# Seven smaller blocks in place of one: the A12 B21 product of a two-level Winograd scheme, with its operand sums on GpSimd

## The chip, the cores and the metric

The kernel runs on one core of one Trainium2 chip. The metric is the device time of one execution in microseconds (us). Matrix products run on TensorE (PE; its weight loads are listed as PEld), elementwise work on VectorE (DVE), ScalarE (ACT) and GpSimd (POOL); DMA transfers are issued from the queue of SyncE (SP). All data is fp32. TensorE writes into PSUM; VectorE and ScalarE take results out of it.

## The reference

Eight batches x[b] of 256 tokens by 1024 features go through two chained products and a residual:

```python
y = einsum('bsi,boi->bso', x, weight[adapter_ids])          # one 1024x1024 matrix per batch
base_out = einsum('btd,od->bto', y, base_W) + base_b        # the same matrix for all batches
logits = einsum('btd,nd->btn', y, router_W) + router_b      # 15 routes; softmax, all ranked, the first 8 kept
h = einsum('btd,erd->bter', y, A)                           # 8 experts of rank 16
lora = einsum('bter,eor->bto', h * w[..., None], B) * 2.0   # w: the weights of the kept routes, mapped to experts
out = x + base_out + lora
```

## The kernel before

**Two phases.** The first computes y, batch by batch, and beside it router and low-rank projections (`project`, L135). The second, from 228 us on, computes the product with base_W for all batches at once, with the low-rank term and the residual added. Both use the Winograd form of Strassen's scheme: a product of two 2 x 2 block matrices made with seven block products instead of eight, at the price of sums of blocks.

**The second phase has two levels.** The outer level is seven products, `seven`, numbered n = 0 to 6 here; the call for n = 6 is `last_product`, the others are `product`. Their right operands are quarters of y held in SBUF: `b11`, `b21`, `b12`, `b22`, some changed in place beforehand by the outer sums (`update`, L812; which product issues which sums is in `sums`). Their left operands (blocks of base_W and sums of them) were prepared in DRAM and are loaded a product ahead by `load_left` (L208, L212), which needs free tiles of the pool `wt` (8 buffers).

**The inner level** is again seven block products, of (256 x 256) by (256 x 1024), hence four matmuls of 128x512 each: left blocks `a11`, `a12`, `a22` and sums `s1` to `s4`, which come from DRAM; right blocks `b11` to `b22` of that product and sums `t1` to `t4`, which VectorE makes (`differences`, L232). Products 1, 3, 5 and 6 also add the low-rank term: inside four of their blocks, two more matmuls each (L587). `half` is one bank's part of a block (L578 for its matmuls). The trace lists every fp32 matmul as two records, so a block of four matmuls shows as x8.

**PSUM and the order of the work.** Each product has three pairs of banks: `pa`, `pb`, `pc`. Winograd's running sums stay in the banks: `pa` collects a11 b11, then + s2 t2, then + s3 t3, then + a22 t4; `pc` collects s1 t1, then + s4 b22. After each block the bank is read (`take`, L630 on ACT in product 5, L634 on ACT in product 0, otherwise on DVE at L607 or, with a bias, L636; `join`, L607 on DVE), and the next block that writes the same bank waits for that read. The order on TensorE is the order of the source, since PE, DVE, ACT and SP are scheduled by hand:

```python
block(pa, a11, b11, True)
block(pc, s1, t1, True, *term(1, 1))
block(pa, s2, t2, False)
block(pb, a12, b21, True, *term(0, 0))
block(pa, s3, t3, False)
block(pc, s4, b22, False, *term(0, 1))
block(pa, a22, t4, False, *term(1, 0))
```

**The gaps.** Between the blocks `gap(k)` issues steps from two queues, `soon` and `later`, two or three at a time (`fill`): the differences for the next product, outer sums, steps of the router's softmax, and the residual sums with their stores (L710, L721, L731, L732, L714). Every engine works strictly through its own list, so a step issued in a gap stands ahead of the next read of a bank on DVE. GpSimd has no work after the first 1.4 us.

**Other tiles the change touches.** `q` (pool of 4 tiles) holds results of products 1 and 5 until they are stored. `late` is a large tile that first holds results of phase one (copied out of it by ACT at L312 until 243.9 us), then, from product 3, results (`v`). `spare` of phase one holds prepared left operands until they are stored to DRAM (L348); the pool `q` lies over it. `ys[0]`, `ys[1]` hold y.

Of the kernel before, what the change touches and what calls it, by code (L numbers as in the profile page):

```python
# [10 lines left out]
F32 = mybir.dt.float32  # L11
# [17 lines left out]
def kernel(  # L29
# [16 lines left out]
    nc = tc.nc  # L46
    P = 128
    B = ids.shape[1]
    S = 256
# [20 lines left out]
    NS = 4  # L70
# [134 lines left out]
    def load_left(n):  # L205

        ra = wpool.tile([P, NS, 4 * P], F32, name="wt")
        nc.sync.dma_start(  # L208
            ra.rearrange("p s f -> p (s f)"), left_raw[n].rearrange("p s f -> p (s f)")
        )  # L210
        su = wpool.tile([P, NS, 3 * P], F32, name="wt")
        nc.sync.dma_start(  # L212
            su.rearrange("p s f -> p (s f)"), left_sum[n].rearrange("p s f -> p (s f)")
        )
        return ra, su

    def quarter(right, i, j):

# [22 lines left out]
    left = {}  # L241
# [307 lines left out]
    with ExitStack() as phase:  # L549
# [9 lines left out]
            tc.tile_pool(name="ps_b", bufs=1, space=bass.MemoryType.PSUM)  # L559
        )  # L560
        phase.enter_context(
            tc.manual_schedule(engines={EN.PE, EN.DVE, EN.Activation, EN.SP})
        )
        add, sub = nc.vector.tensor_add, nc.vector.tensor_sub
        W = 2 * S
# [4 lines left out]
        def fill(n):  # L570
            for _ in range(n):
                if soon or later:
                    (soon or later).popleft()()
# [33 lines left out]
                add(dst[:, mi], accs[mi], base[:, mi])  # L607

        def operands(left, right):
            ra, su = left  # L610
            return (
                [ra[:, :, ts(n, P)] for n in range(4)]
                + [su[:, :, ts(n, P)] for n in range(3)]
                + [quarter(right, i, j) for i in range(2) for j in range(2)]
            )

        def product(left, terms, nexts, right, base, bias, into, done, gaps, u=None, hw=None):

            a11, a12, s3, a22, s1, s2, s4, b11, b12, b21, b22 = operands(left, right)
            t1, t2, t3, t4 = terms

            def take(dst, accs, i, j):
                if bias is None and base is not None:
                    join(dst, accs, base(i, j))
                    return
                for mi in range(2):
                    if bias is None:
                        nc.scalar.copy(dst[:, mi], accs[mi])  # L630
                        continue
                    c = bb[:, bias + 2 * i + mi : bias + 2 * i + mi + 1]
                    if base is None:
                        nc.scalar.activation(dst[:, mi], accs[mi], AF.Identity, bias=c)  # L634
                    else:
                        nc.vector.scalar_tensor_tensor(  # L636
                            dst[:, mi], accs[mi], c, base(i, j)[:, mi], ALU.add, ALU.add
                        )

            def term(i, j):  # L640
                if u is None:
                    return ()
                t = hw[:, j].rearrange("p b t -> p (b t)")
                return (upd[:, u, :] if (i, j) == (0, 1) else up[:, u, i, :]), t

            def gap(n, more=0):
                for step in gaps.get(n, ()):
                    step()
                fill(3 if more and u is not None else 2)

            pa, pb, pc = banks(ps_a, "pa"), banks(ps_b, "pb"), banks(ps_b, "pc")
            c = {ij: into(*ij) for ij in ((0, 0), (1, 1), (0, 1), (1, 0))}
            gap(0)
            block(pa, a11, b11, True)
            take(c[0, 0], pa, 0, 0)
            gap(1, 1)
            block(pc, s1, t1, True, *term(1, 1))
            take(c[1, 1], pc, 1, 1)
            gap(2)
            block(pa, s2, t2, False)  # L660
            take(c[0, 1], pa, 0, 1)
            gap(3, 1)
            block(pb, a12, b21, True, *term(0, 0))
            join(c[0, 0], pb, c[0, 0])
            done(0, 0, c[0, 0])
            gap(4)
            block(pa, s3, t3, False)
            join(c[1, 1], pa, c[1, 1])
            done(1, 1, c[1, 1])
            gap(5, 1)  # L670
            block(pc, s4, b22, False, *term(0, 1))
            join(c[0, 1], pc, c[0, 1])
            done(0, 1, c[0, 1])
            gap(6, 1)
            block(pa, a22, t4, False, *term(1, 0))
            take(c[1, 0], pa, 1, 0)

            while len(nexts) < 4:
                fill(1)
            done(1, 0, c[1, 0])  # L680

        def fresh(i, j):
            return qpool.tile([P, 2, W], F32, name="q")
# [5 lines left out]
            pass  # L689

        u = mpool.tile([P, 2, 2, 2, W], F32, name="u")


        results = [(0, 0), (1, 1), (0, 1), (1, 0)]
# [42 lines left out]
        def last_product(left, terms, right, r, res, u, hw):  # L737


            a11, a12, s3, a22, s1, s2, s4, b11, b12, b21, b22 = operands(left, right)  # L740
            t1, t2, t3, t4 = terms
            pa, pb, pc, pd = (
                banks(p, x) for p, x in ((ps_a, "pa"), (ps_b, "pb"), (ps_b, "pc"), (ps_a, "pa"))
            )
            xl = []

            def ask_all():

                for i in range(2):
                    t = wpool.tile([P, 2, 2 * W], F32, name="wt")  # L750
                    n = number(*r, i, 0)
                    nc.sync.dma_start(t, xr[n : n + 2].rearrange("n p f -> p n f"))
                    xl.append(t)

            def multiply(accs, left, right, first, ij=None):
                t = ()
                if ij is not None:
                    t = (
                        upd[:, u, :] if ij == (0, 1) else up[:, u, ij[0], :],
                        hw[:, ij[1]].rearrange("p b t -> p (b t)"),  # L760
                    )
# [13 lines left out]
            ask_all()  # L775
            multiply(pa, a11, b11, True)
            fill(2)
            take(pa, 0, 0)
            multiply(pc, s1, t1, True, (1, 1))
            fill(3)  # L780
            take(pc, 1, 1)
            multiply(pa, s2, t2, False)
            fill(2)
            take(pa, 0, 1)
            multiply(pc, s4, b22, False, (0, 1))
            fill(3)
# [12 lines left out]
            for acc, mi, at in (  # L799
                (pb[0], 0, ds(0, W)),  # L800
                (pb[1], 1, ds(0, 2 * q)),
                (pd[0], 1, ds(2 * q, q)),
                (pd[1], 1, ds(3 * q, q)),
            ):
                dst = res[:, 0, 0, mi, at]
                half(acc[:, at], mi, a12, b21, True, up[:, u, 0, :], t, at)
                add(dst, acc[:, at], dst)
                nc.sync.dma_start(to[:, mi, at], dst)

        def update(dst, op, x, z, halves=(0, 1)):  # L810
# [12 lines left out]
            (b12, at(u), None, at(u), nothing),  # L823
            (b22, at(u), None, at(v), nothing, 2, hw2),
            (b11, at(u), KH, at(u), nothing),
            (b12, None, None, fresh, joint, 1, hw2),
            (b21, at(u), None, at(u), None, 1, hw1),
        ]

        sums = {  # L830
            0: update(b12, sub, b22, b12, [0]) + update(b12, add, b12, b11, [0]),
            2: update(b11, sub, b12, b11),
            3: update(b21, sub, b21, b12) + update(b12, sub, b22, b12),
        }

        def project_last():
# [9 lines left out]
        for n, (right, base, bias, into, done, *up_hw) in enumerate(seven):  # L846
# [3 lines left out]
            if not last:  # L850
                gaps[0].append(lambda m=n + 1: left.update({m: load_left(lefts[m])}))
                steps = [
                    (lambda s=s: nexts.append(s())) for s in differences(seven[n + 1][0])
                ]
                gaps[0].append(lambda o=steps + sums.get(n, []): soon.extend(o))
            if n == 0:
                for k, count in ((1, 6), (2, 5), (3, 11)):
                    gaps[k].append(lambda count=count: run(behind, count))
# [17 lines left out]
            product(  # L876
                left.pop(n), terms, nexts, right, base, bias, into, done, gaps,
                *(up_hw or (None, None))
            )
            terms = nexts  # L880
# [65 lines left out]
```

## Time and profile before

| | us |
|---|---|
| median of 3 runs (lowest, highest) | 432.93 (432.42, 433.91) |
| the profiled execution | 432.58 |
| its span | 430.8 |
| PE, PEld busy | 425.6, 209.0 |
| DVE, ACT, POOL busy | 327.0, 163.5, 0.7 |
| first matmul of product 0; last matmul's start | 227.96; 427.42 |

Products 0 to 6 start on TensorE at 227.96, 255.92, 286.82, 310.85, 341.75, 365.78 and 396.68 us. The times of a timeline are counted from the start of the span; the profiled execution's own time is 1.8 us more than its span. A group's mean is the duration of one record; matmuls overlap their neighbours, so the time that one takes on the path is read from the distance between starts. The granted TensorE clock is full in all 40 slices.

### The profile page before, as it was taken

How to read it: one execution, taken by the hardware profiler on the slowest of the kernel's cores; microseconds unless marked ns; L12 is line 12 of the kernel's file. 1: busy time of each engine (PE TensorE's matmuls, PEld its weight loads, DVE VectorE, ACT ScalarE, POOL GpSimd, SP SyncE). 2: the span in 40 equal slices, each digit the busy share in tenths (PEclk: the TensorE clock that was granted, in tenths of full speed). 3: DMA queues.
4: the chain of work that ended last, by engine and by line, in shares of the span. 5: the costliest groups of instructions: out<-in, count | busy, mean ns of one | idle time of the engine just before them, and what ended most of it. 6: DMA issues, size and time to landing. Idle time of an engine off the chain costs nothing.

```text
span 430.8 us, 3839 instructions
## 1 busy us (share of the span) xinstructions
PE 425.6 (99%) x1198; PEld 209.0 (49%) x1198; DVE 327.0 (76%) x490; ACT 163.5 (38%) x442; POOL 0.7 (0%) x6
## 2 busy tenths in 40 slices
PE   8999999999999999999999999999999999999997
PEld 6344464644646446455455554444444444444444
DVE  0699999986888898998996477879598495446773
ACT  1019377965758657666826632300000000201000
POOL 0000000000000000000000000000000000000000
PEclk9999999999999999999999999999999999999999
DMA  7997987959788589792694241092702227018525
GB/s 253 417 360 269 345 331 294 315 209 309 233 300 285 213 304 347 241 319 104 224 397 160 97 162 58 2 361 102 267 1 99 73 86 277 2 50 278 202 104 196
DMA packets 26406, 93.13 MB, mean 216 GB/s; under 512 B 2322, under 2 KB 6290, under 8 KB 24082
## 3 DMA queue, kind: packets, MB, share of 16 engines
q1 hardware_dynamic: 26242, 92.36, 59.1%
q10 hardware_dynamic: 144, 0.52, 0.4%
q8 instruction: 9, 0.15, 0.1%
q14 instruction: 11, 0.09, 0.1%
HBM read 71.65 MB, written 21.23 MB: 216 GB/s over the span
## 4 chain that ended last, share of the span: by engine, by line
PE 96%; DMA 2%; SPq 1%; issue 0%; DVE 0%
PE pa L294 24%; PE pa L578 23%; PE pc L294 13%; PE pc L578 11%; PE pb L294 7%; PE ph L135 6%; PE pb L578 5%; PE pc L587 3%; DMA wt<-in_wq_dram 2%; PE pa L587 2%; PE pb L587 1%; PE pa L135 1%; SPq L363 0%; DMA ids_sb<-in_ids_dram 0%; SPq L376 0%
## 5 line engine op out<-in xcount | busy, mean ns | idle before, releaser
L312 ACT COPY y<-late 32x256 f32<-32x256 f32 x256 | 103.0, 402 | 41.9 <-DVE late L247 38.9
L578 PE MATMUL pa<-wt 128*128 128x512 f32 x168 | 76.0, 592 | 0.0
L294 PE MATMUL pa<-wt,x 128*128 128x512 f32 x128 | 57.5, 593 | 0.1
L294 PE MATMUL pa<-wt,tt 128*128 128x512 f32 x120 | 54.0, 593 | 0.0
L578 PEld LDWEIGHTS pa<-wt 128*128 128x128 f32 x168 | 31.9, 190 | 40.2 <-issue 38.5
L630 ACT COPY q<-pa 128x512 f32<-128x512 f32 x6 | 3.5, 586 | 114.4 <-PE pa L578 96.7
L294 PEld LDWEIGHTS pa<-wt,x 128*128 128x128 f32 x128 | 24.2, 190 | 30.4 <-issue 29.9
L258 ACT COPY hwT<-late 32x64 f32<-32x64 f32 x128 | 31.1, 243 | 11.2 <-DVE late L247 9.6
L294 PEld LDWEIGHTS pa<-wt,tt 128*128 128x128 f32 x120 | 22.3, 190 | 26.2 <-issue 25.9
L135 PEld LDWEIGHTS ph<-late,y 128*128 128x128 f32 x224 | 28.4, 189 | 3.3 <-issue 3.3
L294 PE MATMUL pb<-wt,x 128*128 128x512 f32 x64 | 29.1, 595 | 0.8 <-DMA wt<-in_wq_dram 0.8
L294 PE MATMUL pc<-wt,x 128*128 128x512 f32 x64 | 28.9, 594 | 0.0
L294 PE MATMUL pc<-wt,tt 128*128 128x512 f32 x64 | 28.8, 592 | 0.0
L135 PE MATMUL ph<-late,y 128*128 128x143 f32 x224 | 28.6, 284 | 0.0
L578 PE MATMUL pa<-y,wt 128*128 128x512 f32 (+1 forms) x64 | 26.4, 552 | 0.0
L578 PE MATMUL pc<-y,wt 128*128 128x512 f32 x56 | 25.8, 592 | 0.0
L578 PE MATMUL pc<-wt 128*128 128x512 f32 x56 | 25.8, 592 | 0.0
L578 PE MATMUL pb<-y,wt 128*128 128x512 f32 (+1 forms) x56 | 25.0, 577 | 0.0
L409 DVE TENSOR_TENSOR wt<-wt 128x2048 f32<-128x2048 f32 (+1 forms) x9 | 18.4, 2047 | 7.9 <-PE pa L294 5.5
L247 DVE STREAM_TRANSPOSE late<-late 128x512 f32<-128x512 f32 (+1 forms) x33 | 21.4, 647 | 1.1
L294 PEld LDWEIGHTS pb<-wt,x 128*128 128x128 f32 x64 | 12.0, 190 | 16.8 <-issue 14.3
L607 DVE TENSOR_TENSOR u<-pa,u 128x512 f32<-128x512 f32 x20 | 13.4, 686 | 8.3 <-PE pa L578 6.8
(101 smaller groups left out, 453.6 us busy)
## 6 DMA issues: line engine op xcount, KB each, us to landing
wt<-in_wq_dram SPq DMA_DIRECT2D x28, 1024.0 KB, 5.8
x<-in_xq_dram SPq DMA_DIRECT2D x7, 1024.0 KB, 7.3
wt<-left_raw SPq DMA_DIRECT2D x7, 1024.0 KB, 6.7
xt<-in_xr_dram SPq DMA_DIRECT2D x12, 512.0 KB, 4.5
wt<-left_sum SPq DMA_DIRECT2D x7, 768.0 KB, 7.2
wt<-in_wq_dram SPq DMA_DIRECT2D x8, 512.0 KB, 7.8
spare<-in_bq_dram SPq DMA_DIRECT2D x4, 1024.0 KB, 5.1
left_raw<-spare SPq DMA_DIRECT2D x4, 1024.0 KB, 7.3
```

The source lines that it names most:

```text
L135: nc.tensor.matmul(ph[:, j, : ER + N], lhsT=y[:, k // KH, k % KH // 2, th, k % 2, bi, ts(j, P)], rhs=ar_sb[:, k, :], start=(j == order[0] ...
L247: nc.vector.transpose(half, of)
L258: lambda a=a, r=r: nc.scalar.copy(to[32 * r : 32 * r + 32, :, a, :], hw[32 * a : 32 * a + 32, :, ts(r, 32)],)
L294: nc.tensor.matmul(acc, lhsT=right[:, k, :], rhs=left[:, k, :], start=(first and k == 0), stop=(k == KH - 1), skip_group_check=True,)
L312: lambda a=a, r=r: nc.scalar.copy(y[32 * r : 32 * r + 32, :, :, a, :], m[32 * a : 32 * a + 32, :, :, r, :])
L409: nc.vector.tensor_add(q["s1"][:, h], q["a21"][:, h], q["a22"][:, h])
L578: nc.tensor.matmul(acc, lhsT=left[:, 2 * k + mi, :], rhs=right[:, k, at], start=(first and k == 0), stop=(up is None and k == 1), skip_gro ...
L587: nc.tensor.matmul(acc, lhsT=up[:, ts(mi, P)], rhs=hw[:, at], start=False, stop=True, skip_group_check=True,)
L607: add(dst[:, mi], accs[mi], base[:, mi])
L630: nc.scalar.copy(dst[:, mi], accs[mi])
```

## The change

In products 0 to 5 the block A12 B21 is made by Winograd's scheme once more. Its quarters are 128x128 (`d11` to `d22`, of `a12`) and 128x256 (`e11` to `e22`, of `b21`); seven products d e of one 128x256 matmul each take the place of four matmuls of 128x512, with the low-rank term joined to three of them (`ups`, three 128x256 matmuls in place of two of 128x512). The running sum `sx` lives in bank `pb[0]`, the other products one after the other in `pb[1]` (`sy`). Each of the seven results is added by DVE to the quarter of c[0, 0] it belongs to as soon as it is there (`small`), where before two sums of 128x512 joined the whole block.

The sums of the small blocks, four of 128x128 and four of 128x256 in each product and one more 128x128 in products with a low-rank term, are made by GpSimd, which joins the engines scheduled by hand. Those of the left side lie in unused columns of the loaded `su` tile, those of the right side in a place that `room` names: a `q` tile in products 0, 3 and 4, part of `late` in 1 and 2, part of `ys[0]` in 5.

The seven small products stand between the large blocks: two behind a11 b11, two behind s1 t1, two behind s2 t2, one ahead of a22 t4. The block s4 b22 is split into its two halves, one ahead of s3 t3 and one behind it. The number of steps per gap becomes `FILLS`. Product 5 now has its right operand in `b22`, and the two outer sums that were issued in product 3 are issued in products 4 and 5, ahead of the differences.

```diff
-        su = wpool.tile([P, NS, 3 * P], F32, name="wt")
+        su = wpool.tile([P, 4 * NS * P], F32, name="wt")
...
-            tc.manual_schedule(engines={EN.PE, EN.DVE, EN.Activation, EN.SP})
+            tc.manual_schedule(engines={EN.PE, EN.DVE, EN.Activation, EN.SP, EN.Pool})
...
-            def gap(n, more=0):
+            def gap(n):
                 for step in gaps.get(n, ()):
                     step()
-                fill(3 if more and u is not None else 2)
+                fill(FILLS[n] + (u is not None))
...
             gap(0)
+            d11, d21, d12, d22 = (a12[:, n] for n in range(4))
+            e11, e12, e21, e22 = (b21[:, k, ts(h, S)] for k in range(2) for h in range(2))
+            ds1, ds2, ds3, ds4 = (left[2][:, n] for n in range(4))
+            et1, et2, et3, et4 = (home[0][:, ts(n, S)] for n in range(4))
+            plus, minus = nc.gpsimd.tensor_add, nc.gpsimd.tensor_sub
+            plus(ds1, d21, d22)
+            minus(et1, e12, e11)
+            minus(ds2, ds1, d11)
+            minus(et2, e22, et1)
+            minus(ds4, d12, ds2)
+            minus(ds3, d11, d21)
+            minus(et3, e22, e12)
+            minus(et4, e21, et2)
+            if u is not None:
+                ups = [up[:, u, 0, ts(mi, P)] for mi in range(2)]
+                ups.append(home[1])
+                minus(ups[2], ups[0], ups[1])
+            sx, sy = (b[:, :S] for b in pb)
+            def small(acc, d, e, first, mi, h, n=None):
+                joins = u is not None and n is not None
+                nc.tensor.matmul(
+                    acc, lhsT=d, rhs=e, start=first, stop=not joins, skip_group_check=True
+                )
+                if joins:
+                    nc.tensor.matmul(
+                        acc, lhsT=ups[n], rhs=hw[:, 0, h], start=False, stop=True,
+                        skip_group_check=True,
+                    )
+                dst = c[0, 0][:, mi, ts(h, S)]
+                add(dst, acc, dst)
             block(pa, a11, b11, True)
             take(c[0, 0], pa, 0, 0)
-            gap(1, 1)
+            small(sx, d11, e11, True, 0, 0)
+            small(sy, d12, e21, True, 0, 0, 0)
+            gap(1)
             block(pc, s1, t1, True, *term(1, 1))
             take(c[1, 1], pc, 1, 1)
+            small(sy, ds1, et1, True, 1, 1, 1)
+            small(sx, ds2, et2, False, 0, 1)
             gap(2)
             block(pa, s2, t2, False)
             take(c[0, 1], pa, 0, 1)
-            gap(3, 1)
-            block(pb, a12, b21, True, *term(0, 0))
-            join(c[0, 0], pb, c[0, 0])
-            done(0, 0, c[0, 0])
+            small(sy, ds4, e22, False, 0, 1, 2)
+            small(sx, ds3, et3, False, 1, 1)
+            gap(3)
+            half(pc[0], 0, s4, b22, False, *term(0, 1))
+            block(pa, s3, t3, False)
             gap(4)
-            block(pa, s3, t3, False)
+            half(pc[1], 1, s4, b22, False, *term(0, 1))
             join(c[1, 1], pa, c[1, 1])
             done(1, 1, c[1, 1])
-            gap(5, 1)
-            block(pc, s4, b22, False, *term(0, 1))
             join(c[0, 1], pc, c[0, 1])
             done(0, 1, c[0, 1])
-            gap(6, 1)
+            gap(5)
+            small(sx, d22, et4, False, 1, 0, 1)
+            done(0, 0, c[0, 0])
             block(pa, a22, t4, False, *term(1, 0))
+            gap(6)
             take(c[1, 0], pa, 1, 0)
...
+        FILLS = (2, 2, 1, 2, 1, 1, 2)
...
+        def room(n):
+            if n in (1, 2):
+                return late[:, : 4 * S], late[:, 4 * S : 4 * S + P]
+            if n == 5:
+                t = ys[0][:, 0].rearrange("p i j k b t -> p (i j k b t)")
+                return t[:, : 4 * S], t[:, 4 * S : 4 * S + P]
+            q = qpool.tile([P, 2, W], F32, name="q")
+            return q.rearrange("p m t -> p (m t)"), late[:, 16 * S : 16 * S + P]
...
-            (b12, None, None, fresh, joint, 1, hw2),
+            (b22, None, None, fresh, joint, 1, hw2),
...
-            3: update(b21, sub, b21, b12) + update(b12, sub, b22, b12),
+            4: update(b22, sub, b22, b12),
+            5: update(b21, sub, b21, b12),
...
-                gaps[0].append(lambda o=steps + sums.get(n, []): soon.extend(o))
+                ahead = sums.get(n, [])
+                gaps[0].append(
+                    lambda o=ahead + steps if n > 3 else steps + ahead: soon.extend(o)
+                )
```

In `last_product` two counts of steps change: all that is left in `soon` behind the first block, and one step instead of three behind s4 b22.

More of the change, by code (lines that the diff above doesn't have):

```diff
@@ L210, in load_left @@
         )
-        su = wpool.tile([P, NS, 3 * P], F32, name="wt")
-        nc.sync.dma_start(
-            su.rearrange("p s f -> p (s f)"), left_sum[n].rearrange("p s f -> p (s f)")
+        su = wpool.tile([P, 4 * NS * P], F32, name="wt")
+        nc.sync.dma_start(su[:, : 3 * NS * P], left_sum[n].rearrange("p s f -> p (s f)"))
+        return (
+            ra,
+            su[:, : 3 * NS * P].rearrange("p (s f) -> p s f", s=NS),
+            su[:, 3 * NS * P :].rearrange("p (n o) -> p n o", n=4),
         )
-        return ra, su
     def quarter(right, i, j):
@@ L609, in operands @@
         def operands(left, right):
-            ra, su = left
+            ra, su, _ = left
             return (
@@ L615, in operands, with product @@
             )
-        def product(left, terms, nexts, right, base, bias, into, done, gaps, u=None, hw=None):
+        def product(
+            left, terms, nexts, right, base, bias, into, done, gaps, home, u=None, hw=None
+        ):
             a11, a12, s3, a22, s1, s2, s4, b11, b12, b21, b22 = operands(left, right)
@@ L776, in last_product @@
             multiply(pa, a11, b11, True)
-            fill(2)
+            fill(max(2, len(soon)))
             take(pa, 0, 0)
@@ L785, in last_product @@
             multiply(pc, s4, b22, False, (0, 1))
-            fill(3)
+            fill(1)
             take(pc, 0, 1)
@@ L876 @@
             product(
-                left.pop(n), terms, nexts, right, base, bias, into, done, gaps,
+                left.pop(n), terms, nexts, right, base, bias, into, done, gaps, room(n),
                 *(up_hw or (None, None))
```

## The prediction

> **What bounds the kernel now.** I read the page first: the busy times and the chain that ended last.
>
> ```profile
> PE 425.6 (99%) x1198; PEld 209.0 (49%) x1198; DVE 327.0 (76%) x490; ACT 163.5 (38%) x442; POOL 0.7 (0%) x6
> PE 96%; DMA 2%; SPq 1%; issue 0%; DVE 0%
> ```
>
> TensorE is the chain: after a first transfer nothing but matmuls, and no other engine has a share behind it. So what is taken from TensorE is won in full, if no new wait opens; what is added elsewhere costs nothing as long as it comes before the block that needs it. Then I read the busy time of each engine in windows, one per product; products 0, 2 and 4 are the short ones.
>
> ```profile
> core 0: us, PE busy (x) PEld busy (x) DVE busy (x) ACT busy (x) POOL busy (x), PEclk, DMA share, GB/s
> 227.96:255.92 27.96, 27.96 (x91) 14.57 (x90) 17.68 (x37) 14.28 (x33) 0.00 (x0) 1.00 0.30 102
> 286.82:310.85 24.03, 24.03 (x58) 10.64 (x56) 19.14 (x23) 0.00 (x0) 0.00 (x0) 1.00 0.58 221
> 341.75:365.78 24.03, 24.03 (x57) 10.64 (x56) 18.52 (x22) 0.00 (x0) 0.00 (x0) 1.00 0.46 158
> ```
>
> TensorE has no idle time in any of them, at full clock; DVE has 5 to 10 us free in each. Next the timeline of TensorE: the block that goes, in product 2 and with its low-rank term in product 1, and, at the very end, the only matmuls of 256 columns.
>
> ```profile
> 267.93 1.88 PE L578 MATMUL pb<-y,wt 128*128 128x512 f32 x4
> 269.65 1.02 PE L587 MATMUL pb<-hwT,up 128*128 128x512 f32 x2
> ...
> 297.12 3.60 PE L578 MATMUL pb<-y,wt 128*128 128x512 f32 x8
> 300.55 3.60 PE L578 MATMUL pa<-wt 128*128 128x512 f32 x8
> ...
> 425.01 1.03 PE L578 MATMUL pb<-y,wt 128*128 128x256 f32 x4
> 425.87 0.59 PE L587 MATMUL pb<-hwT,up 128*128 128x256 f32 x2
> 426.30 0.61 PE L578 MATMUL pa<-y,wt 128*128 128x128 f32 x4
> ```
>
> From start to start, eight records of 512 columns take 300.55 - 297.12 = 3.43 us, 0.429 each; six of 256 take 426.30 - 425.01 = 1.29, 0.215 each. Half the columns cost half the time: the weight load of each (0.190 by the groups' mean) still hides under 0.215. A matmul is two records: 0.858 and 0.429 us. Last, the groups of DVE at the end of the run and GpSimd's own rows.
>
> ```profile
> L732 DVE TENSOR_TENSOR q<-u,q 128x1024 f32<-128x1024 f32 x4 | 4.9, 1222 | 0.1
> L607 DVE TENSOR_TENSOR u<-pb,u 128x512 f32<-128x512 f32 x2 | 1.4, 686 | 0.4 <-PE pb L578 0.4
> L807 DVE TENSOR_TENSOR u<-pa,u 128x128 f32<-128x128 f32 x2 | 0.6, 292 | 0.6 <-PE pa L587 0.6
> L807 DVE TENSOR_TENSOR u<-pb,u 128x256 f32<-128x256 f32 x1 | 0.4, 425 | 0.6 <-PE pb L587 0.6
> ...
> masks.py:199 POOL TENSOR_SCALAR_AFFINE_SELECT ident<-ident 128x128 f32<-128x128 f32 x1 | 0.3, 294 | 0.1
> ```
>
> **TensorE, what goes and comes.** Four matmuls of 512 (3.43 us) go, seven of 256 (7 x 0.429 = 3.00) come: 0.43 less, six times, 2.57. In products 1, 3 and 5 two more of 512 go (1.72) and three of 256 come (1.29): 0.43 less, three times, 1.29. Together 3.86 us. Splitting s4 b22 moves its halves and adds nothing. More matmuls now begin behind a wait; in the trace the first weight load of a block already waits for a release from DVE or ACT, and TensorE's idle time in the second phase is 0.0 on every line, so a wait that is fulfilled in time costs nothing.
>
> **GpSimd's sums.** No row shows them. From below: DVE's row of the same shapes, 0.43 (128x256) and 0.29 us (128x128). From above: GpSimd's own row of 128x128, 0.294 with one input, doubled for a second input and again for 256 columns: 1.18 and 0.59. I take the upper end, since it is from the engine itself. A product's eight sums are then 4 x 1.18 + 4 x 0.59 = 7.1 us, against 23.6 or more per product. [...]
>
> What matters is when they can start. In product 0 et1 goes into a `q` tile over `spare`, so it waits for the last store from there: issued at 225.52, landed 5.8 us later (the median of that issue alone), 231.3. With 1.18 and 0.59, et1 is there at 232.6, ds2 at 233.2, et2 at 234.4. TensorE wants ds1 and et1 behind a11 b11, two small products and s1 t1: 227.96 + 3.43 + 0.86 + 3.43 = 235.7, and ds2, et2 at 236.1. 1.7 us to spare; the later sums are wanted from 240 on. In product 1 they start when ACT has emptied that part of `late` (243.9 before, some 2 us later now, since s2 t2 ends later), 10 us ahead of their product. In products 2 to 5 they wait for the left tile (loads take about 7 us from the end of product n - 2) and for the places to be free, both in the course of product n - 1: a whole product ahead. Only et4 of product 2 waits for the last small product of product 1, and has 20 us after that. So nothing.
>
> **DVE's reads.** Per product two sums of 512 columns (2 x 0.69) go and seven of 256 (7 x 0.43) come: 1.6 us more on an engine with 5 to 10 free. Each stands right behind its matmul. The second result in `sy` is written a whole s1 t1 after the first is read; the same for the others.
>
> **The large banks.** Less stands between the blocks on `pa` now. s3 t3 follows s2 t2 after two small products and half a block, 0.86 + 1.72 = 2.57 us, where 3.43 stood; `take` of c[0, 1] needs 0.65 behind the end of s2 t2: 1.9 to spare. a22 t4 follows s3 t3 after half a block and one small product, 2.15 us; join needs 0.65: 1.5 to spare. DVE must only not be behind. Put in order for product 2 from the end of a11 b11 (take 1.3 with a lag of 0.7, small sums 0.35 each, two differences 1.14 each, take, small sums, one outer sum), DVE is free at 8.6 us, s2 t2 ends at 8.58. Then two small sums and three outer sums fill the time to 13.4, when half of s3 t3 can be joined since 12.9; s3 t3 ends at 14.6. In product 4 the same places come out within 0.2 us. In products 1, 3 and 5 the blocks are 0.86 to 1.72 us longer and the margins wider. Product 0 takes on ACT: s2 t2 ends at 239.98, and take is done 0.7 later, s3 t3 starts at 242.6. So nothing.
>
> **Queues and what moves.** ACT's copies out of `late` end about 1.7 us later (245.6); the projection that reads them starts behind s4 b22, at 247.7 instead of 245.1. The outer sums moved from product 3 to 4 and 5 are the same eight instructions; in product 4 the first two stand in front of take, where DVE was idle 1.9 us at a time at the end of product 3. On SP the loads of left operands for product 3 stand behind two stores instead of three, those of y's residual in the old order but for one request that goes behind the loads for product 6; the last residual tile comes 4.5 us after about 400, read at 404.6, and the bank that hangs on DVE there (c[0, 1] of product 6) is wanted at 410: the read is done at 408.2. The tail behind product 6's a22 t4 is unchanged.
>
> **The sum.** Profiled 432.58 (span 430.8 and 1.78 around it) less 3.86 is 428.7; the median of three was 0.35 above it, 432.93, hence 429.1.
>
> **Rivals.** [...] Nothing in the trace tells whether GpSimd and DVE disturb each other, as GpSimd never ran beside it. As a mechanism here: each step of DVE with both inputs in SBUF (the 1.22 us rows) and each sum of GpSimd hold each other up for their whole length. In products 2 and 4 two or three sums fall on such steps between s1 t1 and s2 t2, 1.2 to 3.5 us later on DVE against 1.9 to spare: 0 to 1.6 lost in each, 429.1 to 432.3, the middle 430.7. [...]
>
> (2) The other side: GpSimd is far slower than its own row says. In product 0, 231.4 and 2.5 times the duration of a 128x256 sum must not pass 236.1. At 1.9 us TensorE begins to wait, at 3.4 the whole gain is gone, at 4 it waits 5.3 us there and all eight sums (24 us) no longer fit into a short product: 434.4 or more. It needs three times the upper end.
>
> (3) It does not do what it says: matmuls of 256 columns behind waits don't take half. If each small matmul shows its weight load of 0.19, 7 x 6 of them cost 8 us, 437. The rows at the end of the run, each behind other work in the same way, show 0.215.
>
> **How the numbers follow.** Nothing lost 0.72 (428.4 to 430.1, the runs of before lying 0.5 below and 1.0 above their median); a partial loss by (1) 0.15, of which 0.12 ends faster; a gain and a loss that cancel 0.02; (2) 0.07, (3) 0.04. 0.3% of 432.93 is 1.3 us, about what a measurement can tell: faster means under 431.6. Faster 0.84, within 0.05, slower 0.11. The range 428.4 to 431.0 holds the first case and the lower part of (1).
>
> **What would show it.** Right: the seven windows of TensorE 23.6 and 30.0 us long (product 0 27.5), no idle on PE, rows of 128x256 with 0.215 from start to start, POOL some 18 to 45 us busy and ahead of PE. Wrong by (2): PE idle at the third and fourth small product, released by POOL, first at 235.7. Wrong by (1): the 1.22 us rows of DVE longer or later, PE idle at s3 t3, released by DVE. Wrong by (3): small matmuls 0.4 us apart with PEld between. An idle at a22 t4 would mean that I put DVE's order too early.

## The result, and the profile after

| | before | changed |
|---|---|---|
| median of 6 runs (lowest, highest), us | 432.85 (432.42, 433.91) | 430.25 (429.60, 431.54) |
| profiled execution, its span, us | 432.58, 430.8 | 430.95, 429.2 |
| ratio of the medians (95% interval) | | 0.9942 (0.9924 to 0.9961) |

The change gains 2.60 us, 0.6%. Forecast were 3.86 us and 429.1; the sign and the range (428.4 to 431.0) held, the size did not. From the page of the changed kernel come the line of busy time by engine and that of the chain that ended last.

```profile
PE 423.7 (99%) x1246; PEld 218.0 (51%) x1246; DVE 338.0 (79%) x520; ACT 163.7 (38%) x442; POOL 35.3 (8%) x57
PE 91%; DVE 4%; DMA 4%; SPq 1%; issue 0%; DVEq 0%
```

TensorE is still the bound: 99% busy, 1.9 us less than before. GpSimd has 34.6 us more to do, DVE 11.0. In the chain DVE now has 4% where it had none, and DMA 4% where it had 2%: in this execution the chain runs, near the end, through something other than matmuls. The busy time of each engine, product by product, says where (a row: window, its length, busy time of each engine with its instructions, granted clock, DMA).

```profile
core 0: us, PE busy (x) PEld busy (x) DVE busy (x) ACT busy (x) POOL busy (x), PEclk, DMA share, GB/s
228.33:255.87 27.54, 27.54 (x96) 15.70 (x95) 16.33 (x39) 14.52 (x33) 9.63 (x17) 1.00 0.44 163
255.87:286.37 30.50, 30.50 (x84) 15.58 (x82) 26.44 (x45) 8.35 (x33) 5.09 (x7) 1.00 0.00 1
286.37:309.99 23.62, 23.62 (x63) 11.78 (x62) 23.48 (x31) 0.00 (x0) 7.79 (x9) 1.00 0.44 166
309.99:340.49 30.50, 30.50 (x84) 15.58 (x82) 16.55 (x25) 0.00 (x0) 4.89 (x9) 1.00 0.51 190
340.49:364.11 23.62, 23.62 (x63) 11.78 (x62) 21.86 (x29) 0.00 (x0) 6.41 (x8) 1.00 0.04 11
364.11:394.61 30.50, 30.50 (x84) 15.58 (x82) 22.42 (x28) 4.10 (x7) 0.00 (x0) 1.00 0.44 154
394.61:425.78 31.17, 31.09 (x84) 14.63 (x82) 22.77 (x28) 0.59 (x1) 0.00 (x0) 1.00 0.66 246
```

The row of product 1 in the kernel before:

```profile
255.92:286.82 30.90, 30.90 (x74) 13.68 (x73) 23.72 (x40) 8.34 (x33) 0.00 (x0) 1.00 0.33 124
```

The lengths before were 27.96, 30.90, 24.03, 30.90, 24.03, 30.90, and 30.74 for product 6 up to its last matmul. So products 0 to 5 gain 0.40 to 0.42 each, 2.44 together, and TensorE is busy for the whole of each window. Forecast for products 1, 3 and 5 were 30.0: they came out at 30.50, and gain no more than the products without a low-rank term. Product 6, whose matmuls are unchanged, is 0.43 longer. With the start of product 0, here 0.37 later (228.33 against 227.96; it lies between 227.46 and 229.21 over the profiles of this study, all with the same first phase), the sum is 2.44 - 0.43 - 0.37 = 1.64, which is the difference of the two profiled executions but for 0.01.

**The low-rank matmuls.** The groups of L688, the joined low-rank matmuls, in the changed kernel (records; busy time and mean of one; idle time before them):

```profile
L688 PE MATMUL pb<-hwT,up 128*128 128x256 f32 x18 | 5.4, 379 | 0.0
L688 PE MATMUL pb<-hwT,late 128*128 128x256 f32 x4 | 1.2, 379 | 0.0
L688 PE MATMUL pb<-hwT,y 128*128 128x256 f32 x2 | 0.6, 379 | 0.0
```

Their places in TensorE's timeline in product 1 (start, duration, records):

```profile
260.17 0.59 PE L688 MATMUL pb<-hwT,up 128*128 128x256 f32 x2
...
266.18 0.59 PE L688 MATMUL pb<-hwT,up 128*128 128x256 f32 x2
...
270.91 0.59 PE L688 MATMUL pb<-hwT,late 128*128 128x256 f32 x2
...
280.79 0.59 PE L688 MATMUL pb<-hwT,up 128*128 128x256 f32 x2
```

18 + 4 + 2 = 24 records are 12 matmuls, four in each of three products. The list `ups` has three entries, but the calls of `small` in the diff name n = 0, 1, 2 and, for d22 et4, 1 again. Where the section on the change says "joined to three of them", it must say four. Four matmuls of 256 columns cost what the two of 512 cost that went. The first line of the page shows the same: 1246 - 1198 = 48 records more, which is 6 x (14 - 8) for the small products and 3 x (8 - 4) for the low-rank term; with three it would be 42.

**Product 6.** DVE's timeline in the changed kernel (in brackets the idle time before a row, and what ended it):

```profile
404.05 1.28 DVE L610 TENSOR_TENSOR u<-pc,u 128x512 f32<-128x512 f32 x2
409.00 1.23 DVE L783 TENSOR_TENSOR q<-q,xt 128x1024 f32<-128x1024 f32 x1 [3.67 <-DMA xt<-in_xr_dram]
410.14 1.22 DVE L831 TENSOR_TENSOR u<-u,wt 128x1024 f32<-128x1024 f32 x1
411.28 1.28 DVE L610 TENSOR_TENSOR u<-pa,u 128x512 f32<-128x512 f32 x2
```

TensorE's timeline at the block s3 t3, in the same execution:

```profile
410.92 1.02 PE L590 MATMUL pc<-hwT,upd 128*128 128x512 f32 x2
412.02 2.41 PE L581 MATMUL pa<-wt 128*128 128x512 f32 x5
```

The weight loads at s3 t3 and at the next block, a22 t4, with what released them:

```profile
412.02 0.30 PEld L581 LDWEIGHTS pa<-wt 128*128 128x128 f32 x2 [0.91 <-DVE u L610]
415.54 0.30 PEld L581 LDWEIGHTS pa<-wt 128*128 128x128 f32 x2 [0.65 <-DVE u L610]
```

The last residual tile was requested at 402.27 us and landed 6.6 us later, at 408.9. In DVE's list the step that reads it and one more stand ahead of the `take` of c[0, 1], and s3 t3 waits for that `take`: it starts 1.10 us after the matmul pair before it, where 0.86 is the distance without a wait. The other 0.19 of the 0.43 us is lost at a22 t4, which waits for DVE's read of s3 t3's bank; DVE is still late there and ends that read at 415.49. From the start of s3 t3 to the first low-rank matmul of a22 t4 it is 5.34 us, against 5.15 before.

**GpSimd and DVE beside each other.** GpSimd's timeline in the changed kernel, sums made during product 4 (start, duration):

```profile
345.58 0.46 POOL L671 TENSOR_TENSOR wt<-wt 128x128 f32<-128x128 f32 x1
345.99 1.44 POOL L672 TENSOR_TENSOR wt<-wt 128x128 f32<-128x128 f32 x1
347.39 1.71 POOL L673 TENSOR_TENSOR y<-y 128x256 f32<-128x256 f32 x1
349.06 0.72 POOL L674 TENSOR_TENSOR y<-y,y 128x256 f32<-128x256 f32 x1
```

DVE's timeline at the same time, two outer sums:

```profile
345.74 2.77 DVE L875 TENSOR_TENSOR y<-y 128x1024 f32<-128x1024 f32 x2
```

Three groups of DVE in the changed kernel (records; busy time, mean of one in ns; idle time before them):

```profile
L235 DVE TENSOR_TENSOR wt<-y,wt 128x1024 f32<-128x1024 f32 x14 | 17.6, 1255 | 0.2
L875 DVE TENSOR_TENSOR y<-y,y 128x1024 f32<-128x1024 f32 x12 | 16.4, 1396 | 0.0
L610 DVE TENSOR_TENSOR u<-pa,u 128x512 f32<-128x512 f32 x20 | 13.2, 682 | 3.1 <-PE pa L581 1.5 <-PE pa L590 1.5
```

The second of them in the kernel before, where GpSimd has no work:

```profile
L812 DVE TENSOR_TENSOR y<-y,y 128x1024 f32<-128x1024 f32 x12 | 14.2, 1216 | 0.0
```

Undisturbed, a sum of GpSimd takes 0.45 us (128x128) or 0.73 (128x256), inside the forecast's bounds (0.29 to 0.59 and 0.43 to 1.18). Beside a step of DVE that reads two tiles from SBUF it takes up to 1.44 and 1.71: 0.99 and 0.98 more, where two such steps alone take 2.27 from start to start (254.22 to 256.49), 1.14 each. Such steps grow too: the outer sums (L812, now L875) from 1216 to 1396 ns on average, and a difference that starts at 281.17, beside a sum from 281.10 on, takes 1.74 us instead of 1.22. Reads of a bank, with one input in PSUM, are not longer: 682 ns, and 686 before; two of them at 298.88 take 1.27 us together, as others do, and the sum of 128x256 that starts at 299.23 beside them takes 0.72. So in these rows the steps that the prediction's first rival names hold each other up, and reads of a bank and sums do not.

### The profile page after: what moved, and what is told of

It reads as the page before. It is cut to its first block, busy times and chain, and to the rows that moved or that the text cites. A ratio compares the mean times of both kernels' runs of the same rounds, so it can differ in the third digit from the quotient of the medians.

```text
span 429.2 us, 4059 instructions
## 1 busy us (share of the span) xinstructions
PE 423.7 (99%) x1246; PEld 218.0 (51%) x1246; DVE 338.0 (79%) x520; ACT 163.7 (38%) x442; POOL 35.3 (8%) x57
## 4 chain that ended last, share of the span: by engine, by line
PE 91%; DVE 4%; DMA 4%; SPq 1%; issue 0%; DVEq 0%
PE pa L297 24%; PE pa L581 20%; PE pc L297 13%; PE pc L581 10%; PE pb L297 7%; PE ph L135 6%; PE pb L684 4%; PE pc L590 2%; DMA wt<-in_wq_dram 2%; DMA out_dram<-q 1%; PE pa L590 1%; DVE q L794 1%; PE pb L688 1%; DVE late L793 1%; PE pa L135 1%; DVE q L783 1%
## 5 line engine op out<-in xcount | busy, mean ns | idle before, releaser
L667 POOL TENSOR_TENSOR wt<-wt 128x128 f32<-128x128 f32 x6 | 3.1, 512 | 261.3 <-DVE spare L341 219.5
L297 PEld LDWEIGHTS pc<-wt,x 128*128 128x128 f32 x64 | 12.1, 190 | 15.5 <-issue 14.8
```

What stands on the lines that cost most here:

```text
L297: nc.tensor.matmul(acc, lhsT=right[:, k, :], rhs=left[:, k, :], start=(first and k == 0), stop=(k == KH - 1), skip_group_check=True,)
```

## The experiments

Each kernel is the changed one with the edit shown. Lengths of products are distances between first matmuls on TensorE, as above. Each ratio is against runs of the kernel before on the same chip; their medians were 432.46, 432.45 and 432.50 (21, 21 and 19 runs).

Theory A: the low-rank term saves nothing, so every product gains 0.40 to 0.42, and what is moved costs up to 0.4 in product 6. Rival B is the prediction's account: products 1, 3 and 5 should gain 0.86 each, and if they don't, something has taken half of it back. Rival C: the sums on GpSimd take it back, by way of the slower steps of DVE.

### Seven small blocks in products 1, 3 and 5 alone

```diff
+            seven_small = u is not None
...
             take(c[0, 1], pa, 0, 1)
-            small(sy, ds4, e22, False, 0, 1, 2)
-            small(sx, ds3, et3, False, 1, 1)
+            if seven_small:
+                small(sy, ds4, e22, False, 0, 1, 2)
+                small(sx, ds3, et3, False, 1, 1)
+            else:
+                block(pb, a12, b21, True, *term(0, 0))
+                join(c[0, 0], pb, c[0, 0])
```

The sums and the other small products are put under `if seven_small` in the same way.

> The changed kernel, with the seven small blocks in products 1, 3 and 5 alone (those with a low-rank term); in products 0, 2 and 4 A12 B21 is one block again, behind s2 t2. My corrected account (four 256-column low-rank matmuls cost as much as the two of 512 that went, so each product gains one eighth of a block, 0.43 us, with or without that term): products 1, 3, 5 last 30.5 us on TensorE, 0 and 2 and 4 as before (27.96, 24.03), the gain is 1.29 us less what product 6 loses, 431.6 to 432.0. The account of the prediction (0.86 in each product with a low-rank term): those products 30.0 us, a gain of 2.57, 430.3.

Measured: 431.70 us (431.19 to 432.08, 11 runs), ratio 0.9978 (0.9969 to 0.9987). Products 1 and 2 by windows of busy time, columns as above:

```profile
256.09:286.59 30.50, 30.50 (x83) 15.58 (x82) 25.76 (x46) 8.35 (x33) 0.00 (x0) 1.00 0.01 2
286.59:310.62 24.03, 24.03 (x57) 10.64 (x56) 22.14 (x26) 0.00 (x0) 5.83 (x9) 1.00 0.47 174
```

Products 1, 3 and 5 are 30.50 long here too, products 2 and 4 are 24.03 as before. In product 1 GpSimd does nothing at all (its sums ran in product 0), so the sums can't be taking a gain back there, and TensorE has no idle time in it. B falls: with the low-rank term the gain is 0.40 each, and nothing has taken any back. The median gained only 0.76 where the three windows give 1.20, though in the profile product 6 lost nothing (30.74); that rest is taken up in the last pair of experiments.

### One block everywhere, no sums on GpSimd

The kernel of the first experiment, with:

```diff
-            seven_small = u is not None
+            seven_small = False
```

> The changed kernel with A12 B21 as one block in all products and without GpSimd's sums; the halves of s4 b22 around s3 t3, the counts of steps, the moved outer sums and the late joining of c[0, 0] stay. If the loss of 0.43 us in product 6 comes from what is moved and not from the small blocks: products 0 to 5 as before on TensorE, product 6 still 0.2 to 0.5 us longer than the 30.74 before, the last residual tile landing after 406; time 432.9 to 433.4. If it comes from the small blocks or GpSimd: product 6 as before, 432.9 or slightly under.

Left of the change are the order of the blocks, the steps per gap, the moved outer sums and the later store of c[0, 0]. Measured: 432.84 us (432.19 to 433.20, 11 runs), ratio 1.0008 (0.9999 to 1.0017), 0.06 below the range expected. Products 0 to 5 are as long as before (27.95, 30.90, 24.04, 30.90, 24.03, 30.90), product 6 is 31.15 against 30.74. DVE's timeline at the last residual tile:

```profile
410.55 1.23 DVE L792 TENSOR_TENSOR q<-q,xt 128x1024 f32<-128x1024 f32 x1 [3.17 <-DMA xt<-in_xr_dram]
```

The group of the outer sums in the same kernel:

```profile
L884 DVE TENSOR_TENSOR y<-y,y 128x1024 f32<-128x1024 f32 x12 | 14.1, 1217 | 0.0
```

So the loss in product 6 comes from what is moved and not from the small blocks, and without sums on GpSimd DVE's steps are back at 1217 ns.

### The last product's residual steps issued later

```diff
             multiply(pa, s2, t2, False)
-            fill(2)
             take(pa, 0, 1)
             multiply(pc, s4, b22, False, (0, 1))
-            fill(1)
+            fill(3)
```

This is done to the changed kernel, to the one-block kernel, and, beside them, the changed kernel runs once more as it is.

> The changed kernel, but in the last product the two steps that stood ahead of the read of c[0, 1] (the fourth residual sum of product 5 and one of its own) stand behind it. If the wait for the last residual tile is what TensorE loses in product 6: no idle ahead of s3 t3, product 6 is 30.7 us again, 0.2 to 0.45 us faster than the changed kernel, 429.8 to 430.05. If the loss is something else (the bank, the transfer rate): the same 430.2 to 430.3.

> The changed kernel as it is, once more, to stand beside the others on the same chip. All accounts: 430.25 within 0.4; product lengths on TensorE 27.5, 30.5, 23.6, 30.5, 23.6, 30.5 us; product 6 30.7 to 31.2.

> A12 B21 as one block in all products (as in the run before), and the two steps of the last product behind the read of c[0, 1]. If what that run lost to the kernel before (0.38 us at the median) is the wait for the last residual tile in product 6: 0.4 less, at the kernel before within 0.1%, product 6 at 30.74 us. If it is spread over the products or lies in the first phase: still 0.3 to 0.4 slower than the kernel before.

| kernel | us (lowest, highest, runs) | ratio (95% interval) | product 6 | DVE's wait for the tile |
|---|---|---|---|---|
| changed, again | 430.02 (429.50, 430.35, 5) | 0.9938 (0.9924 to 0.9952) | 30.76 | 3.24 |
| changed, late steps | 430.05 (429.89, 430.44, 5) | 0.9943 (0.9930 to 0.9957) | 30.74 | 0.89 |
| one block | 432.84 (432.19, 433.20, 11) | 1.0008 (0.9999 to 1.0017) | 31.15 | 3.17 |
| one block, late steps | 432.49 (432.15, 433.06, 11) | 1.0004 (0.9995 to 1.0013) | 30.74 | 1.05 |

DVE's step on that tile in the timeline of the changed kernel, run again:

```profile
408.13 1.22 DVE L783 TENSOR_TENSOR q<-q,xt 128x1024 f32<-128x1024 f32 x1 [3.24 <-DMA xt<-in_xr_dram]
```

The same in the kernel with one block and late steps:

```profile
410.49 1.22 DVE L792 TENSOR_TENSOR q<-q,xt 128x1024 f32<-128x1024 f32 x1 [1.05 <-DMA xt<-in_xr_dram]
```

With one block the late steps take the loss away in the profile (0.41) and, by the medians of two chips, in time: 0.38 above the kernel before without them, 0.04 with them; the two intervals overlap. In the changed kernel they bring nothing that can be measured, a miss for an expected 0.2 to 0.45: in this second profile the step on the tile starts 0.87 us earlier than in the first, 0.42 earlier counted from the start of product 6, which is just in time, and product 6 lost 0.02. So the wait is real, but whether it costs anything is settled by some tenths of a microsecond in the landing, from one execution to the next. The changed kernel run again gains 2.44 us by the medians and 2.45 by its windows of products 0 to 5; that the two agree so closely is chance, since the interval of the ratio allows 2.1 to 3.3 us.

### Each sum on GpSimd three times, and five times

```diff
-            plus, minus = nc.gpsimd.tensor_add, nc.gpsimd.tensor_sub
+            def plus(*of):
+                for _ in range(3):
+                    nc.gpsimd.tensor_add(*of)
+
+            def minus(*of):
+                for _ in range(3):
+                    nc.gpsimd.tensor_sub(*of)
+
```

> The changed kernel with each of GpSimd's sums made three times over (the same result). By the margins read from the trace (0.73 and 0.45 us a sum; in product 0 the first right-hand sum starts 3.7 us after the product does, ds2 and et2 are wanted 8.2 us after it): 2 x 2.2 + 1.35 puts et2 at 9.5, TensorE waits about 1.3 us at the third and fourth small product of product 0, released by GpSimd, and nowhere else through the sums being late; more two-input steps of DVE meet a sum, which costs at most 0.5 in products 2 and 4. 431.2 to 432.0. If the sums have no margin (a product's sums are the bound): five to ten us more. If they have more than I read: 430.0 to 430.3 as without the repeats.

Measured: 434.77 us (434.60 to 434.98, 4 runs), ratio 1.0057 (1.0042 to 1.0072): some 3 us above the expectation. TensorE's only idle times in the second phase, from its timeline:

```profile
238.22 0.70 PE L691 MATMUL pb<-q,wt 128*128 128x256 f32 x2 [1.49 <-POOL q L672]
243.65 0.70 PE L691 MATMUL pb<-q,wt 128*128 128x256 f32 x2 [0.86 <-POOL q L672]
298.30 1.10 PE L691 MATMUL pb<-late,wt 128*128 128x256 f32 x4 [1.07 <-DVE u L700]
```

DVE's timeline ahead of the third of them (two rows between the first and the second are left out):

```profile
288.55 3.41 DVE L790 TENSOR_TENSOR q<-q,xt 128x1024 f32<-128x1024 f32 x2
...
294.46 1.63 DVE L235 TENSOR_TENSOR wt<-y,wt 128x1024 f32<-128x1024 f32 x1
296.02 1.28 DVE L610 TENSOR_TENSOR u<-pa,u 128x512 f32<-128x512 f32 x2
297.21 0.94 DVE L700 TENSOR_TENSOR u<-pb,u 128x256 f32<-128x256 f32 x2
```

Product 0 lost 2.89 us and product 2 lost 1.32. In product 0 I had reckoned with et2 alone; et3 came late as well. From start to start each of the three waits costs 0.25 to 0.27 us more than the idle time that the row gives. Product 2 is rival C: the steps of DVE with two inputs take up to 1.74 us instead of 1.22 there, and five of them ahead of the read of a small product (L700) add up to the 1.8 us by which it comes later in the product than in the changed kernel. The next small product, which goes into the same half bank `sy`, waits. So C's mechanism is real, and at the single dose it costs TensorE nothing: no idle time in product 2, 23.62 us.

With `range(5)` in the same edit:

> The same with each sum five times. By the margins: 2 x 3.65 + 2.25 puts et2 at 13.3 us, a wait of 5.1 us in product 0, 24 us of sums in each product, still made ahead of the others; 435 to 437. If GpSimd's whole time per product were the bound, products 2 and 4 would grow too, 440 or more.

Measured: 491.18 us (490.87 to 492.17, 4 runs), ratio 1.1368 (1.1350 to 1.1385). The lengths are 38.40, 45.67, 24.63, 47.41, 23.63, 47.80 and 30.73. The longest wait, in product 1, from TensorE's timeline:

```profile
293.61 1.22 PE L695 MATMUL pb<-hwT,late 128*128 128x256 f32 x2 [12.14 <-POOL late L672]
```

Windows around it (the granted clock is the last column but two):

```profile
281.50:293.60 12.10, 0.00 (x0) 0.00 (x0) 0.87 (x2) 0.00 (x0) 10.93 (x20) 0.65 0.01 1
293.60:298.50 4.90, 4.89 (x8) 2.86 (x9) 3.11 (x12) 0.00 (x0) 4.35 (x9) 0.50 0.00 0
299.00:304.00 5.00, 5.00 (x14) 2.13 (x13) 3.45 (x6) 3.85 (x16) 4.61 (x8) 1.00 0.00 0
```

GpSimd's timeline, ten of the 128x128 sums of product 2 in a row:

```profile
308.30 10.49 POOL L672 TENSOR_TENSOR wt<-wt 128x128 f32<-128x128 f32 x10
```

GpSimd is the bound here, as in the second of the two cases expected: it works without a pause from 231.4 to 437.1 us. But the loss is far above the 440 named there, and products 2 and 4, which were to grow too, did so by 1.0 us and not at all. Three things belong to it. The sums themselves grow beside DVE: the ten above take 1.05 us each, where the five of `ups[2]` in product 1 (2.58 us from 290.98 on) take 0.52, and the forty sums of product 2 run for 37.5 us where the undisturbed durations give 23.6. What TensorE waits for at 281 us is the ninth sum, `ups[2]`: it stands last in GpSimd's list, behind et4, though its matmul comes third of the four (what an earlier place would be worth, no run here shows).

And each long wait costs twice: TensorE's idle times add up to 44.9 us of the 61 lost, and after each of five waits of 3.4 to 12.1 us the granted clock is 0.50 for 4.5 to 6.2 us (in the rows above until some 298.7), an estimated 2.6 us lost each time (half of that), 13 in all. Of the remaining 3 us, an estimated 2 are what the nine waits cost from start to start beyond their listed idle time (up to 0.27 each, as above). After a wait of 1.49 us in the run before this one the clock stayed at 1.00; after one of 1.62 us in this one the next four records of 512 columns took 1.71 us (251.40 to 253.11), the 0.43 each of full clock.

### The sums on VectorE

```diff
-            plus, minus = nc.gpsimd.tensor_add, nc.gpsimd.tensor_sub
+            plus, minus = add, sub
```

> The changed kernel with the eight sums of each product on VectorE, at the same place of the source (ahead of the read of the first block). By my account of DVE: 2.5 us more per product on an engine that stands in order, where product 2 leaves 1.9 us and product 4 2 us ahead of s3 t3: 0 to 1.5 us lost in each of these two, none in 1, 3, 5; 430.3 to 433. If only the eighth of the matmuls counts and DVE has room: 430.0. If DVE had been as tight as its busy share of 79% suggests: over 433.

Measured: 431.33 us (430.91 to 432.14, 10 runs), ratio 0.9975 (0.9966 to 0.9985), so 1.3 us slower than the changed kernel. The one idle time that TensorE's timeline lists in the second phase:

```profile
295.54 1.13 PE L684 MATMUL pb<-late,wt 128*128 128x256 f32 x4 [0.84 <-DVE u L693]
```

DVE's timeline ahead of it, where the last of the sums is the first row:

```profile
293.00 0.42 DVE L674 TENSOR_TENSOR late<-y,late 128x256 f32<-128x256 f32 x1
293.34 1.28 DVE L610 TENSOR_TENSOR u<-pa,u 128x512 f32<-128x512 f32 x2
294.54 0.94 DVE L693 TENSOR_TENSOR u<-pb,u 128x256 f32<-128x256 f32 x2
```

Product 2 is 24.73 long instead of 23.62; products 0, 1, 3, 4 and 5 keep the gain, and product 6 is 30.84. I had expected the wait at s3 t3; it is at the third small product, as in the kernel with three sums: the same margin, used up by 2.2 us of sums on DVE. So GpSimd is worth 1.3 us here by the medians of two chips; 1.11 of it is seen in the profile, in one product of six.

### Even products and odd products

The first experiment and its opposite, both with the late steps, so that the wait in product 6 is out of the comparison; the second kernel differs from the first by:

```diff
-            seven_small = u is not None
+            seven_small = u is None
```

> Seven small blocks in products 1, 3 and 5 alone, and the late step of the last product put right. Windows: 30.50 for products 1, 3 and 5, the other lengths as before, 30.74 for product 6: 1.2 us less than before in all, so 431.2 to 431.4. If the half microsecond that the run without the late step lacked against its windows was the wait for the last residual tile in most executions, this kernel is 0.3 to 0.45 us faster than that one; if it was something else, it stays at 431.7. By the prediction's account of the low-rank term (0.86 per product, and so 2.6 in all) it would be 429.9.

> Seven small blocks in products 0, 2 and 4 alone (no low-rank term, and in products 1, 3 and 5 one block behind s2 t2), with the late step put right. Windows: 27.54, 23.62 and 23.62 for products 0, 2 and 4 and 30.90 for the others: 1.25 us less than before, 431.2. By the prediction's account these products are worth 0.43 each too, 1.29; so here the two accounts agree, and the sum of this gain and that of the other three products must give that of the whole change (2.4 to 2.6) by the one account, 3.9 by the other.

| seven small blocks in | us (lowest, highest, runs) | ratio (95% interval) | products 0 to 5 | median span | time outside the span |
|---|---|---|---|---|---|
| none (the kernel before) | 432.50 (431.54, 433.04, 19) | 1 | 168.72 | 430.7 | 1.74 to 1.82 |
| 1, 3, 5 | 431.68 (431.23, 433.11, 12) | 0.9983 (0.9974 to 0.9992) | 167.52 | 429.6 | 2.02 to 2.11 |
| 0, 2, 4 | 431.61 (430.73, 431.88, 7) | 0.9973 (0.9963 to 0.9984) | 167.48 | 429.6 | 1.95 to 2.18 |

By the windows the two halves gain 1.20 and 1.24, and 1.20 + 1.24 = 2.44 is what the whole change gains. The medians gain less, 0.82 and 0.89, and the odd half with late steps is no faster than without: that the missing half microsecond was the wait for the tile is refuted. Most of it lies outside the profiled span. The time of an execution less its span was 1.95 to 2.18 us in all 30 runs of the three kernels that mix both kinds of product, and 1.73 to 1.87 in the runs of all other kernels here. The spans themselves gain 1.1 and 1.1. Why a mixed program has 0.3 us more outside its span is not shown by anything here, and stays open.

## Why the prediction was right or wrong

**The low-rank term, wrong.** The step that failed is this one of the sum: "In products 1, 3 and 5 two more of 512 go (1.72) and three of 256 come (1.29): 0.43 less, three times, 1.29". Four come, so 1.72 go and 1.72 come, and the term is 0. The rest of the sum stands: 3.86 - 1.29 = 2.57, against 2.44 by the windows and by the second set of runs and 2.60 by the first; with the term at 0 the forecast would have been 430.4. It was a miscount from the diff, not a matter of the chip, and in products 0 to 5 no wait or engine took a gain back. That the result lies in the range is luck in this respect: the upper part of the range was put there for rival (1), not for a miscount. Its lower end is 0.2 below what it is said to come from (429.1 less 0.5 is 428.6); nothing hangs on that.

**The price of a small matmul, right.** Seven of 256 columns take seven times 0.43 us, at places with waits too; rival (3) falls. It was also priced at half: 0.19 us is the weight load of one record, and 42 matmuls are 84 records, 16 us. Each product gained 0.40 to 0.42 where 0.43 was the sum; the 0.01 to 0.03 between them are not accounted for.

**GpSimd in time, right.** In product 0 et1 started at 232.07 (forecast 231.3) and et2 was done at 233.90, 2.6 us ahead of its matmul where 1.7 was the forecast, since the sums were shorter than the upper end that I took. Rival (2) put the start of the wait for et2 at a 128x256 sum of 1.9 us, and the repeated sums bear that out: at 2.34 us (0.78 each) its reckoning gives 231.4 + 2.5 x 2.34 - 236.1 = 1.2 us of wait there, and 1.49 were measured. But it left out et3 and product 2, so three times the measured length cost 4.2 us in the windows (4.7 by the medians) where it gave 1.2, and five times cost 61.

**GpSimd and DVE beside each other, rival (1): the mechanism is there, its price is not.** Steps of DVE with two inputs in SBUF grew by 3.0 us in all (2.2 and 0.3 in the outer sums, 0.5 in the differences), single ones from 1.22 to 1.81. The reads of the banks that count were still in time. With the sums made three times, it costs 1.32 us in product 2, where the rival put it, but at the third small product and not at s3 t3; product 4 lost nothing. It was not decided by sums running while DVE waits: in product 2 there is hardly any such time (DVE 23.48 busy of 23.62, and 21.86 in product 4). What decided, by the runs that use it up, is the slack of the single reads: in product 2 sums three times over and sums on DVE both exhaust it, at the same small product.

**The last residual tile, wrong in its size.** Forecast was a landing 4.5 us after about 400, and the bank wanted at 410. The request went out at 402.27, behind the store of the joint sums, and took 6.6 us. The 1.8 us that I left as slack (408.2 against 410) were less than the error of the two numbers together, 4.3 us; the bank itself was wanted later than forecast too, at 411.8. It cost 0.43 us in one profile and 0.02 in the other.

**The order of the blocks, DVE's reads and the tail, right.** With one block in the new order, products 0 to 5 keep their old lengths to 0.01 us, so the split s4 b22, the moved outer sums and the steps per gap cost TensorE nothing there. DVE's reads of the small products cost nothing either: in the changed kernel TensorE is busy for the whole of products 0 to 5. From the start of the last matmul to the end of the span it is 3.4 us before and after.

## What to carry to other kernels

Count what a diff issues call by call, from the calls and not from the length of a list that they index, and set the count against the number of instructions: here 48 more records instead of 42 name the error at once. Where a change is worth 0.4 us per stage, the distances between the first matmuls of the stages settle it to 0.02 us, when medians scatter by more than that and hold things that are no part of the stage. A margin for work on a second elementwise engine must be reckoned with the longer durations that both engines have beside each other (here up to 1.71 us instead of 0.73, and 1.81 instead of 1.22), and a slack behind a transfer with the slowest landing in the trace (7.0 us for a residual tile in the kernel before), not the median (4.5).

## What the runs showed of the hardware that I had not expected

- GpSimd's sums and DVE's steps with two inputs in SBUF lengthen each other, and the sums more: 0.45 to 1.44 us and 0.73 to 1.71, on DVE 1.22 to 1.81. The undisturbed rows of GpSimd give 0.28 us for 128 more columns, 2.2 ns each.
- Five waits of TensorE, of 3.4 to 12.1 us, were each followed by 4.5 to 6.2 us at a granted clock of 0.50, which adds an estimated 2.6 us to their price; waits of 1.49 and 1.62 us were not.
- The time outside the span differs by program, in every run: 1.95 to 2.18 us for the three kernels that mix two kinds of product, 1.73 to 1.87 for all others, also on the same chip. The cause stays open.
